# Two transformer-like layers on one core: layer 0's pairs of query tiles in another order on fixed PSUM banks, norms by a power, strips without fills, and the last pair's tail written out

## The chip, the cores and the metric

The kernel runs on one core of a Trainium2 chip, in fp32. The core has a matrix engine (TensorE, "PE"), a vector engine ("DVE"), an activation engine ("ACT"), a general engine ("POOL") and a queue engine ("SP") that issues most DMAs. Each engine works through its own instructions in order. Matmul results land in PSUM, which this kernel uses as eight banks of 128x512 floats. The metric is device time in microseconds (us); lower is better.

## The reference

The input x has shape (4, 2048, 256): four sequences of 2048 tokens. Two layers follow one another, each on a layer norm of its input and each added to that input.

```python
xn = _layernorm(x, axis=-1)
x = x + _L0_attn_ref(xn, ...) + _L0_ffn_ref(xn, ...)
xn = _layernorm(x, axis=-1)
x = x + _L1_attn_ref(xn, ...) + _L1_ffn_ref(xn, ...)
```

- The layer norm subtracts the mean and divides by sqrt(variance + 1e-5).
- Layer 0, first part: a gated linear recurrence along time, with a[t] and b[t] from two sigmoid gates of xn.
- Layer 0, second part: a router takes the mean over time of xn @ Wr + br, a softmax, and picks 4 of 16 heads (head size 64). For these four heads it computes full softmax attention over the 2048 keys (queries, keys and values scaled by the gate g), and multiplies by Wo.
- Layer 1, first part: causal attention with 16 heads of size 16 over 2048 tokens, then W_o.
- Layer 1, second part: a channel mix, sigmoid(xr @ W_r^T) * (relu(xk @ W_k^T)^2 @ W_v^T), where xr and xk mix a token with the one before.

## The kernel before

The four sequences (batches) are computed one after another. Every engine's program order is the order in which the Python code issues instructions; no planner moves them. The code interleaves work by generators: `steps(stream, n)` runs a stream n yields further. The streams are `recurring` (the recurrence, called `background` inside `attention0`), `projecting` (queries and keys of the next head), `rest_of_values` (values of layer 0), `norming` (the norm that layer 1 reads), `opening` (projections and strips of layer 1) and `leading` (row maxima of layer 1).

**Banks.** `own_bank` hands the eight banks out in turn. While `summing` is on, bank 7 is left out, because the weighing of layer 0 accumulates in it. A matmul that gets a bank must wait until the last reader of that bank is done.

**Layer 0's attention** (`attention0`) loops over 32 pairs of query tiles of 128 tokens (4 heads, 8 pairs each) plus two extra rounds that finish the last pairs. A pair has two tiles, a and c. For each tile:
- `scores` (L498): four matmuls (eight instructions in the trace, which shows two for each but a transpose) of 64 rows against 512 keys, two at a time on the two halves of the array, into four banks; DVE takes the maximum of each bank (L502) and joins them, negated, to `nm` (L506);
- `exponentials` (L512): ACT computes exp(score - max) of each bank into `p`, and sums rows on the way;
- `turn` (L520): PE transposes p, sixteen 128x128 blocks into four banks; `keep` (L526) copies each bank to `pT`, two on DVE and two on ACT;
- `weigh` (L545): for both tiles together, 64 instructions of pT with the values, in two halves (`weigh(0)`, `weigh(1)`) into bank 7; `weighed` (L552) copies the result on ACT;
- `project` (L558) multiplies by Wo, and `add` (L563) adds to x on DVE, divided by the row sum.

These steps are spread over rounds of the loop: in round n the code turns tile c of pair n-1 (`late`), projects pair n-2 (`older`), computes the scores of pair n, weighs pair n-1 and turns tile a of pair n. The order of a round is: late's turn, project, a's scores, c's first half of scores, weigh half, c's second half, weigh half, a's turn. The first round of a batch also computes values (L446) and the last steps of the recurrence: `added` (L330) on DVE, and transposes of y (L337) which are added to x.

**Norms** (`Norm`): `stats` (L257, L258 on DVE) per tile; `root` (L261) takes a square root on ACT; `inverse` (L265) a reciprocal on DVE; `rows` (L272) normalizes on DVE; `turn` (L278) transposes on PE and copies (L279). The norm of layer 1 runs inside `attention0` from the last head's pair 3 on, in blocks of four tiles (`all_blocks`), and ends in the two extra rounds and the eight rounds after them. The norm of the next batch runs inside layer 1 (`prepared`). [...]

**Layer 1** keeps q and k of four heads in a "strip": a tile with head h at partitions 32h to 32h+15. `open` (L711) fills a q strip with zeros and a k strip with ones on POOL; `copy` (L717) copies 16 rows per head by DMA. Row 16 of each head of the q strip later gets the negated row maximum by DMA, and meets a row of ones in k, so the matmul itself subtracts the maximum. `Maxima` (L772, L775, L778) compute row maxima of scores; `Weights` (L797 scores, L799 exp, L802 causal mask on POOL, L808 weighing, L814 copy, L815 sum on POOL) the attention, with a division of the result at L891 on POOL. `Leading.lead` issues one unit of four maxima.

## Time and profile before

| what | us |
|---|---|
| runs: median (lowest to highest of three) | 4234.19 (4233.68 to 4235.58) |
| profiled execution, own time | 4234.65 |
| its span in the trace | 4232.9 |
| first pair of layer 0 of each batch begins (L498) | 99.8, 1145.9, 2189.4, 3233.5 |
| PE busy | 4129.7 (98%) |
| DVE busy | 3107.5 (73%) |
| ACT busy | 2797.4 (66%) |
| POOL busy | 1044.9 (25%) |
| period of an ordinary pair of layer 0 | 11.82 |

Busy time is the sum of an engine's own instructions. A timeline row gives a start and a length in us, the engine, the line of the kernel, the operation with output <- inputs and the shape, and how many instructions the row stands for; in brackets comes the idle time before it and what ended it. Matmuls of different rows of the array overlap, so a row's length may be more than the distance to the next start. A row of waits gives the waiting instruction, what it waited for, the total in us, how often, and the longest. A row of windows gives for each engine the busy us and number of instructions, then the granted clock of PE as a share of full speed.

### The profile page before, as it was taken

To read this page: it belongs to the slowest core of one execution; us is meant where nothing else is said; L and a number is where in the kernel's file an instruction comes from. 1 tells how busy PE (TensorE), PEld (TensorE's weight loads), DVE (VectorE), ACT (ScalarE), POOL (GpSimd) and SP (SyncE) were. 2 spreads that over 40 slices of the span, in tenths; PEclk is the share of its full clock that TensorE was granted. 3 is DMA by queue.
4 is the path that set the end of the run, shared out by engine and by line. 5 is a ranking of instruction groups with operands and counts; after the bars stand their busy time and mean duration, and the time that the engine had idled before them with its cause. 6 is when DMAs were issued, how large, how long until landed. Compare 5 with 4: busy or idle time off the path is not lost.

```text
span 4232.9 us, 86387 instructions
## 1 busy us (share of the span) xinstructions
PE 4129.7 (98%) x32994; PEld 2283.5 (54%) x32994; DVE 3107.5 (73%) x7292; ACT 2797.4 (66%) x6388; POOL 1044.9 (25%) x1322
## 2 busy tenths in 40 slices
PE   6999999999999999999999999999999999999998
PEld 3777643334477764333457776433446777643334
DVE  5777778887577777888657776888856767688882
ACT  3666648886566665888656665688865666568874
POOL 0000015544100002654410000265440000036544
PEclk9999999999999999999999999999999999999999
DMA  3000010100100001110010000011000000001000
GB/s 87 1 11 1 6 18 17 19 25 17 27 1 11 1 6 19 17 37 6 19 25 1 11 1 9 16 17 37 7 19 23 1 11 1 16 11 17 16 7 24
DMA packets 70819, 65.80 MB, mean 16 GB/s; under 512 B 37234, under 2 KB 58628, under 8 KB 68868
## 3 DMA queue, kind: packets, MB, share of 16 engines
q1 hardware_dynamic: 66624, 57.19, 6.2%
q8 instruction: 260, 4.26, 0.4%
q10 hardware_dynamic: 3780, 3.07, 0.3%
q14 instruction: 155, 1.27, 0.1%
HBM read 16.70 MB, written 8.39 MB: 6 GB/s over the span
## 4 chain that ended last, share of the span: by engine, by line
PE 90%; DVE 5%; ACT 2%; issue 1%; POOL 1%; DMA 1%; ACTq 0%; SPq 0%; POOLq 0%; DVEq 0%
PE bank L797 15%; PE bank L772 13%; PE bank L808 12%; PE bank L520 11%; PE bank L498 10%; PE bank L545 10%; PE bank L993 4%; PE bank L703 3%; PE bank L294 3%; PE bank L558 2%; DVE mx L778 1%; PE bank L477 1%; PE bank L460 1%; PE bank L981 1%; DVE mx L502 1%; ACT p L512 1%
## 5 line engine op out<-in xcount | busy, mean ns | idle before, releaser
L799 ACT ACTIVATE p<-bank 128x512 f32<-128x512 f32 (+3 forms) x2560 | 1175.4, 540 | 281.1 <-PE bank L797 146.5
L772 PE MATMUL bank<-k,q 32*128 32x512 f32 (+3 forms) x5120 | 1139.1, 564 | 3.2 <-DVE mx L778 1.3
L778 DVE TENSOR_REDUCE mx<-bank 128x1 f32<-128x512 f32 x1536 | 952.9, 682 | 239.0 <-PE bank L772 238.6
L797 PE MATMUL bank<-q,k 32*128 32x512 f32 (+3 forms) x5120 | 1089.6, 555 | 0.0
L512 ACT ACTIVATE p<-bank,nm 128x512 f32<-128x512 f32 x1024 | 689.5, 685 | 568.6 <-DVE nm L506 568.5
L815 POOL TENSOR_TENSOR o<-o,w 128x512 f32<-128x512 f32 (+3 forms) x576 | 627.6, 1090 | 757.5 <-ACT w L814 752.0
L502 DVE TENSOR_REDUCE mx<-bank 128x1 f32<-128x512 f32 x1024 | 645.3, 681 | 94.8 <-PE bank L498 94.2
L797 PEld LDWEIGHTS bank<-q,k 32*128 32x128 f32 x5120 | 418.4, 184 | 533.7 <-ACT p L799 445.5
L808 PE MATMUL bank<-p,v 128*17 128x512 f32 (+3 forms) x5120 | 602.9, 534 | 16.6 <-POOL p L802 11.7
L526 DVE COPY pT<-bank 128x512 f32<-128x512 f32 x512 | 352.6, 691 | 293.2 <-PE bank L520 277.6
L545 PEld LDWEIGHTS bank<-pT,v 128*64 128x64 f32 x8192 | 441.9, 137 | 189.8 <-issue 189.3
L498 PE MATMUL bank<-k,q 64*128 64x512 f32 x2048 | 542.5, 611 | 0.8
L775 DVE CUSTOM_DVE_ANT_0 bank<-bank,cmask 128x512 f32<-128x512 f32 (+3 forms) x1024 | 473.3, 521 | 75.0 <-PE bank L772 56.4
L520 PE MATMUL bank<-ident,p 128*128 128x128 f32 x4096 | 492.3, 275 | 19.9 <-ACT p L512 19.7
L545 PE MATMUL bank<-pT,v 128*64 128x128 f32 x8192 | 503.7, 276 | 0.0
L772 PEld LDWEIGHTS bank<-k,q 32*128 32x128 f32 x5120 | 426.7, 183 | 136.7 <-DVE mx L778 34.5
L520 PEld LDWEIGHTS bank<-ident,p 128*128 128x128 f32 x4096 | 445.3, 141 | 73.8 <-ACT p L512 29.8
L711 POOL MEMSET q<- 128x2048 f32 x16 | 28.9, 1804 | 1659.5 <-PE bank L545 1659.5
L814 ACT COPY w<-bank 128x512 f32<-128x512 f32 (+3 forms) x576 | 305.1, 530 | 101.9 <-PE bank L808 68.4
L526 ACT COPY pT<-bank 128x512 f32<-128x512 f32 x512 | 293.4, 600 | 63.5 <-PE bank L520 61.5
L808 PEld LDWEIGHTS bank<-p,v 128*17 128x17 f32 x5120 | 89.7, 95 | 431.1 <-ACT p L799 235.8
L498 PEld LDWEIGHTS bank<-k,q 64*128 64x128 f32 x2048 | 210.5, 188 | 170.7 <-issue 84.9
(164 smaller groups left out, 3354.8 us busy)
## 6 DMA issues: line engine op xcount, KB each, us to landing
x<-in_L_attn_x_dram SPq DMA_DIRECT2D x20, 512.0 KB
q<-q SPq DMA_DIRECT2D x64, 128.0 KB
vals<-o SPq DMA_DIRECT2D x256, 32.0 KB
out_dram<-x SPq DMA_DIRECT2D x32, 256.0 KB
q<-qp SPq DMA_DIRECT2D x48, 128.0 KB
k<-kp SPq DMA_DIRECT2D x48, 128.0 KB
q<-nmT SPq DMA_DIRECT2D x256, 2.0 KB
q<-qp SPq DMA_DIRECT2D x64, 32.0 KB
```

Source lines behind the costliest of these rows:

```text
L498: PE.matmul(self.s[j][i], lhsT=self.qT[i][half_, self.t * P:(self.t + 1) * P], rhs=self.kT[half_, j * QB:(j + 1) * QB], start=True, stop=True)
L502: DVE.tensor_reduce(self.mx[:, n:n + 1], self.s[j][i], AX.X, ALU.max)
L512: ACT.activation(self.p[j][:, i, :], self.s[j][i], AF.Exp, bias=nm, accum_out=self.sums[:, n:n + 1])
L520: PE.transpose(self.tr[j][i][:, n * P:(n + 1) * P], self.p[j][:, i, n * P:(n + 1) * P], ident)
L526: copy(self.pT[:, n0:n0 + 4, :], self.tr[j][i].rearrange("p (n q) -> p n q", q=P))
L545: PE.matmul(acc[i * DH:(i + 1) * DH, 0:P], lhsT=self.v[h][:, N * j + n, self.k * DH:(self.k + 1) * DH], rhs=tile_.pT[:, 8 * h + N * j + n, ...
L772: PE.matmul(s[:, 0:n], lhsT=self.qT[strip(h), self.qs], rhs=self.kT[strip(h), self.ks], start=True, stop=True)
L778: DVE.tensor_reduce(self.mx[:, h, :], s[:, 0:n], AX.X, ALU.max)
L797: PE.matmul(s[:, c0:QB], lhsT=self.kT[strip(h), self.ks], rhs=self.qT[strip(h), self.q0 + c0:self.q0 + QB], start=True, stop=True)
L799: ACT.activation(p[:, h % 2, c0:QB], s[:, c0:QB], AF.Exp, scale=SC1)
L808: PE.matmul(acc[32 * h:32 * h + DH1 + 1, c0:QB], lhsT=self.v[h], rhs=self.p[h // 2][:, h % 2, c0:QB], start=True, stop=True)
L815: POOL.tensor_tensor(self.o[:, c0:QB], self.o[:, c0:QB], w[:, c0:QB], ALU.add)
```

## The change

The change has five parts.

1. *Norms by a power.* `root` and `inverse` become one step: DVE adds epsilon to the variance and POOL raises it to the power -0.5. The constant for epsilon goes; a constant of -0.5 comes. Over the whole program 39 of 58 table loads on ACT go.
2. *The router's mean.* The weight of 1/T becomes a tile of ones, and the factor 1/T moves into DVE's addition of the bias.
3. *Pairs in another order, on fixed banks.* `scores`, `turn`, `weigh` and `project` get their banks as arguments. Of late's four blocks of transposes, one comes first, and the other three between a's scores and c's scores. c's scores are no longer split, and the weighing is one run of 64 instructions into bank 0 after them. Late's four copies are all on ACT (before, two on DVE), which is 256 copies over the program. Streams that run inside a round are lent banks 6 and 4 at its start, and 4 and 7 at its end (1 and 3 in the first round). The first round runs no background step; values run two blocks and two blocks. The norm gets four steps per round; `all_blocks` has other yields.
4. *The last pair's tail.* The two extra rounds become straight code after the loop. In it, the maxima of layer 1 are issued as one unit, two units, and eight units in a loop, 11 in all before layer 1 begins (13 before), and the norm's steps stand among them.
5. *Strips without fills.* The maxima read 16 rows of a strip and the weights 17, instead of 32. POOL's fills go (32 of 1.8 us); the ones of the k strips come by DMA from the tile of ones, ahead of the copies (28 DMAs over the program).

```diff
@@ -112,10 +112,14 @@
-    turn, summing = [0], [False]
+    turn, summing, lent = [0], [False], []
...
+        if lent:
+            lent.append(lent.pop(0))
+            return banks[lent[-1]]
@@ -140,15 +144,15 @@
-    mean_w = const.tile([P, P], FP, tag="mean_w", name="mean_w")
-    POOL.memset(mean_w, 1.0 / T)
+    ones = const.tile([P, P], FP, tag="ones", name="ones")
+    POOL.memset(ones, 1.0)
...
-    eps_c = const.tile([P, 1], FP, tag="eps", name="eps_c")
-    POOL.memset(eps_c, EPS)
+    minus_half = const.tile([P, NT], FP, tag="minus_half", name="minus_half")
+    POOL.memset(minus_half, -0.5)
@@ -257,12 +261,10 @@
-        def root(self, t, n):
-            ACT.activation(self.rs[:, t:t + n], self.mv[:, t:t + n, 1:2].rearrange("p n o -> p (n o)"),
-                           AF.Sqrt, bias=eps_c)
...
-            DVE.reciprocal(self.rs[:, t:t + n], self.rs[:, t:t + n])
+            rs = self.rs[:, t:t + n]
+            DVE.tensor_scalar(rs, self.mv[:, t:t + n, 1:2].rearrange("p n o -> p (n o)"), EPS, None, ALU.add)
+            POOL.tensor_tensor(rs, rs, minus_half[:, 0:n], ALU.pow)
@@ -354,9 +356,9 @@
-            PE.matmul(ps[:, 0:NH], lhsT=mean_w, rhs=ws[:, c, :], start=(c == 0), stop=(c == 1))
+            PE.matmul(ps[:, 0:NH], lhsT=ones, rhs=ws[:, c, :], start=(c == 0), stop=(c == 1))
...
-        DVE.tensor_tensor(dist, ps[:, 0:NH], br_b, ALU.add)
+        DVE.scalar_tensor_tensor(dist, ps[:, 0:NH], 1.0 / T, br_b, ALU.mult, ALU.add)
@@ -491,8 +493,8 @@
-        def scores(self, j):
-            self.s[j] = [bank() for _ in range(2)]
+        def scores(self, j, to):
+            self.s[j] = to
@@ -501,29 +503,28 @@
-        def exponentials(self, js):
-            nm = sm.tile([P, 1], FP, tag="nm0", name=f"nm0_{self.name}")
-            DVE.tensor_reduce(nm, self.mx, AX.X, ALU.max, negate=True)
+        def maximum(self):
+            self.nm = sm.tile([P, 1], FP, tag="nm0", name=f"nm0_{self.name}")
+            DVE.tensor_reduce(self.nm, self.mx, AX.X, ALU.max, negate=True)
...
-            for j in js:
...
+        def exponentials(self, j, i):
+            if j not in self.p:
...
-                for i in range(2):
-                    n = 2 * j + i
-                    ACT.activation(self.p[j][:, i, :], self.s[j][i], AF.Exp, bias=nm,
-                                   accum_out=self.sums[:, n:n + 1])
...
-        def turn(self, j):
...
-            self.tr[j] = [bank() for _ in range(2)]
-            for i in range(2):
-                for n in range(4):
-                    PE.transpose(self.tr[j][i][:, n * P:(n + 1) * P], self.p[j][:, i, n * P:(n + 1) * P], ident)
+            n = 2 * j + i
+            ACT.activation(self.p[j][:, i, :], self.s[j][i], AF.Exp, bias=self.nm, accum_out=self.sums[:, n:n + 1])
...
+        def turn(self, j, i, to):
...
+            self.tr[j, i] = to
+            for n in range(4):
+                PE.transpose(to[:, n * P:(n + 1) * P], self.p[j][:, i, n * P:(n + 1) * P], ident)
...
-            copy(self.pT[:, n0:n0 + 4, :], self.tr[j][i].rearrange("p (n q) -> p n q", q=P))
+            copy(self.pT[:, n0:n0 + 4, :], self.tr[j, i].rearrange("p (n q) -> p n q", q=P))
@@ -537,22 +538,22 @@
-        def weigh(self, j):
-            acc, N = banks[7], NT // 4
-            for n in range(N):
+        def weigh(self, acc):
+            self.acc = acc
+            for n in range(NT // 2):
...
-                                  lhsT=self.v[h][:, N * j + n, self.k * DH:(self.k + 1) * DH],
-                                  rhs=tile_.pT[:, 8 * h + N * j + n, :], start=(j == n == h == 0),
-                                  stop=(j == h == 1 and n == N - 1))
+                                  lhsT=self.v[h][:, n, self.k * DH:(self.k + 1) * DH],
+                                  rhs=tile_.pT[:, 8 * h + n, :], start=(n == h == 0),
+                                  stop=(h == 1 and n == NT // 2 - 1))
...
-            ACT.copy(self.o, banks[7][:, 0:P])
...
-        def project(self):
-            self.ps = [bank() for _ in range(2)]
+            ACT.copy(self.o, self.acc[:, 0:P])
...
+        def project(self, to):
+            self.ps = to
@@ -562,6 +563,14 @@
+        def share(self):
+            for tile_ in self.tiles:
+                tile_.share()
...
+        def stats(self, norm):
+            for tile_ in self.tiles:
+                norm.stats(tile_.t)
@@ -569,33 +578,39 @@
         older, before = None, None
-        summing[0] = True
...
                 yield
-                norm.root(4 * q, 4)
-                yield
                 norm.inverse(4 * q, 4)
+                yield
                 norm.rows(q, 0, 2)
...
                     norm.turn(q, c, ACT.copy)
-                    yield
-                yield
-                yield
-        for n in range(NA * NP + 2):
+                    if q == NQ - 1:
+                        yield
+                yield
+                yield
+                yield
+                yield
+        def lend(*which):
+            lent[:] = which
+        def of(*which):
+            return [banks[i] for i in which]
+        for n in range(NA * NP):
             k, i = divmod(n, NP)
-            if i == 0 and 0 < k < NA:
+            if i == 0 and k:
                 steps(projecting, 100)
                 qk = following
-            new = Pair0(b, k, i, *qk, v, xt) if k < NA else None
-            a, c = new.tiles if new else (None, None)
+            new = Pair0(b, k, i, *qk, v, xt)
+            a, c = new.tiles
             if i == NP - 3 and k + 1 < NA:
@@ -606,82 +621,106 @@
-            steps(background, 1)
+            late = before.tiles[1] if before else None
+            lend(6, 4)
+            if n:
+                steps(background, 1)
             steps(projecting, 1)
...
-            if n in (NA * NP - 3, NA * NP - 1) or n >= NA * NP:
+            if n in (NA * NP - 3, NA * NP - 1):
                 steps(opening, 2)
-            if n >= NA * NP:
-                leading.lead()
+            lend()
             if before:
-                late = before.tiles[1]
-                late.turn(1)
-                late.turn(0)
-                late.keep(1, 0, DVE.tensor_copy)
-                late.keep(0, 0, DVE.tensor_copy)
-                late.keep(0, 1, ACT.copy)
+                late.turn(1, 1, *of(7))
                 late.keep(1, 1, ACT.copy)
-                for tile_ in before.tiles:
-                    tile_.share()
-            steps(background, 1)
+            if older:
+                older.project(of(3, 2))
+            if before:
+                before.share()
+            if older:
+                older.add()
+                if n - 2 >= (NA - 1) * NP:
+                    older.stats(norm)
+            steps(norming, 1)
+            a.scores(0, of(0, 5))
+            a.scores(1, of(4, 7))
+            a.maximum()
+            if before:
+                for j, i, to in ((0, 0, 1), (0, 1, 3), (1, 0, 6)):
+                    late.turn(j, i, *of(to))
+                    late.keep(j, i, ACT.copy)
+            else:
+                lend(1, 3)
+                steps(rest_of_values, 2)
+                lend()
+            for j, i in ((0, 0), (1, 1), (1, 0), (0, 1)):
+                a.exponentials(j, i)
+            steps(norming, 1)
+            c.scores(1, of(2, 1))
+            c.scores(0, of(3, 6))
+            c.maximum()
+            if before:
+                before.weigh(banks[0])
+            c.exponentials(0, 0)
+            c.exponentials(1, 1)
+            if before:
+                before.weighed()
+            c.exponentials(1, 0)
+            c.exponentials(0, 1)
+            lend(4, 7)
+            steps(rest_of_values, 2)
+            if n:
+                steps(background, 1)
             steps(projecting, 1)
             steps(norming, 1)
-            if older:
-                older.project()
-                older.add()
-                if n - 2 >= (NA - 1) * NP:
-                    for t in range(2):
-                        norm.stats(2 * (n - 2 - (NA - 1) * NP) + t)
-            if before and new is None:
-                leading.lead()
-            if new:
-                a.scores(0)
-                a.scores(1)
-                a.exponentials((0, 1))
-                steps(rest_of_values, 4)
-            steps(norming, 1)
-            if new:
-                c.scores(1)
-            if n >= NA * NP:
-                steps(opening, 1)
-            if before:
-                if new is None:
-                    leading.lead()
-                before.weigh(0)
-            if new:
-                c.scores(0)
-                c.exponentials((1, 0))
-            if before:
-                if new is None:
-                    leading.lead()
-                before.weigh(1)
-            if new:
-                a.turn(1)
-                a.turn(0)
-                a.keep(1, 0, DVE.tensor_copy)
-                a.keep(0, 0, DVE.tensor_copy)
-                a.keep(1, 1, ACT.copy)
-            if before:
-                before.weighed()
-            if new:
-                a.keep(0, 1, ACT.copy)
-            steps(norming, 1)
+            lend()
+            for j, i, to, copy in ((0, 0, 5, DVE.tensor_copy), (1, 0, 3, DVE.tensor_copy),
+                                   (1, 1, 0, ACT.copy), (0, 1, 1, ACT.copy)):
+                a.turn(j, i, *of(to))
+                a.keep(j, i, copy)
             older, before = before, new
...
+        summing[0] = True
+        steps(norming, 1)
+        steps(opening, 2)
+        leading.lead()
+        late = before.tiles[1]
+        for j, i in ((1, 1), (0, 0), (0, 1), (1, 0)):
+            late.turn(j, i, own_bank())
+            late.keep(j, i, ACT.copy)
+        older.project([own_bank() for _ in range(2)])
+        before.share()
+        older.add()
+        older.stats(norm)
+        steps(norming, 1)
+        for _ in range(2):
+            leading.lead()
+        steps(norming, 1)
+        before.weigh(banks[7])
+        before.weighed()
+        steps(norming, 1)
+        steps(opening, 1)
+        before.project([own_bank() for _ in range(2)])
+        before.add()
+        before.stats(norm)
+        steps(norming, 4)
+        steps(opening, 3)
         summing[0] = False
         for _ in range(8):
-            steps(opening, 1)
             leading.lead()
             steps(norming, 1)
+            steps(opening, 1)
         steps(norming, 100)
...
-    def strip(h):
-        return slice(32 * h, 32 * h + 32)
+    def strip(h, rows):
+        return slice(32 * h, 32 * h + rows)
@@ -706,11 +745,11 @@
-            t = half_tile(f"{'qk'[i]}1_{self.b}_{g}")
-            self.strips.setdefault(g, []).append(t)
-            POOL.memset(t, (0.0, 1.0)[i])
+            self.strips.setdefault(g, []).append(half_tile(f"{'qk'[i]}1_{self.b}_{g}"))
...
+            n = (blk.stop - blk.start) // P
+            SP.dma_start(self.strips[g][1][DH1:P:32, blk].rearrange("h (a r) -> h a r", r=P), ones[0:4 * n, :])
@@ -769,7 +808,7 @@
-            PE.matmul(s[:, 0:n], lhsT=self.qT[strip(h), self.qs], rhs=self.kT[strip(h), self.ks],
+            PE.matmul(s[:, 0:n], lhsT=self.qT[strip(h, DH1), self.qs], rhs=self.kT[strip(h, DH1), self.ks],
@@ -794,8 +833,8 @@
-            PE.matmul(s[:, c0:QB], lhsT=self.kT[strip(h), self.ks],
-                      rhs=self.qT[strip(h), self.q0 + c0:self.q0 + QB], start=True, stop=True)
+            PE.matmul(s[:, c0:QB], lhsT=self.kT[strip(h, DH1 + 1), self.ks],
+                      rhs=self.qT[strip(h, DH1 + 1), self.q0 + c0:self.q0 + QB], start=True, stop=True)
@@ -1024,9 +1063,8 @@
-            norm.root(0, NT)
+            norm.inverse(0, NT)
...
-            norm.inverse(0, NT)
```

## The prediction

> **What bounds the kernel now.** I read the page's busy times and its chain first, then TensorE's (PE's) waits, then timelines around the largest ones.
>
> ```profile
> PE 4129.7 (98%) x32994; PEld 2283.5 (54%) x32994; DVE 3107.5 (73%) x7292; ACT 2797.4 (66%) x6388; POOL 1044.9 (25%) x1322
> ...
> PE 90%; DVE 5%; ACT 2%; issue 1%; POOL 1%; DMA 1%; ACTq 0%; SPq 0%; POOLq 0%; DVEq 0%
> ```
>
> PE is busy for 98% and makes 90% of the chain. So an edit counts only where it removes PE time or PE waiting. The waits that belong to the changed code:
>
> ```profile
> PE bank L520 <- ACT p L512: 19.7, 16, 1.3
> PE bank L337 <- DVE y L330: 18.9, 4, 4.7
> PE bank L808 <- POOL p L802: 11.7, 20, 1.3
> ```
>
> (us in total, times, longest.) The first two are 38.6 us. The 4.7 us wait comes once per batch, in the first pair:
>
> ```profile
> 1144.92 1.09 PE L337 MATMUL bank<-ident,y 128*128 128x128 f32 x4 [4.73 <-DVE y L330]
> 1145.93 3.78 PE L498 MATMUL bank<-k,q 64*128 64x512 f32 x8
> 1149.64 7.17 PE L446 MATMUL bank<-wv,xT 128*128 128x256 f32 x32
> 1156.75 1.99 PE L498 MATMUL bank<-k,q 64*128 64x512 f32 x8
> ...
> 1161.45 0.66 PE L520 MATMUL bank<-ident,p 128*128 128x128 f32 x4 [1.25 <-ACT p L512]
> ```
>
> Eight L498 matmuls take 3.78 us here and 1.99 us ten us later. The windows (the last columns are granted clock, DMA share, GB/s) say why: the clock falls to about half after the wait.
>
> ```profile
> 1140.00:1145.00 5.00, 0.27 (x2) 0.12 (x2) 4.96 (x5) 0.38 (x1) 0.00 (x0) 0.78 0.00 0
> 1145.00:1150.00 5.00, 5.00 (x14) 2.12 (x15) 3.20 (x5) 0.00 (x0) 0.00 (x0) 0.54 0.01 3
> 1278.30:1302.00 23.70, 23.70 (x236) 17.59 (x236) 18.38 (x41) 15.62 (x43) 0.00 (x0) 1.00 0.00 1
> ```
>
> The last row is two ordinary pairs: PE never idles, full clock, 11.82 us a pair. The late pairs have stalls from the norm's square root, which stands between two tiles' exponentials:
>
> ```profile
> 1502.49 1.28 ACT L261 ACT_TABLE_LOAD   x1
> 1503.79 0.30 ACT L261 ACTIVATE rs<-mv,eps_c 128x4 f32<-128x4 f32 x1
> 1504.10 1.28 ACT L512 ACT_TABLE_LOAD   x1
> ```
>
> **Start of a batch (pair 0): 6.5 us gained, four times.** The late steps of recurrence (the L330 adds and the first L337 block) leave pair 0. Before, PE was done with earlier values at 1140.2 and reached pair 1's scores at 1165.35: 25.2 us. After, the same stretch by the rows: a's scores 1140.2–1142; then two blocks of values on banks 1 and 3, held until DVE's copy of the previous block has emptied one: that copy starts at 1142.91 (the scan on DVE is ahead of it) and takes 0.67, so a new wait of 1.6; values to 1147.1 (half of 7.17); c's scores to 1149; a wait of 0.4 for bank 4, which a's third exponential reads; values to 1153; a's turn to 1154.9. That is 14.7, 10.5 less, but work is only put off: 12 late transposes (1.3) and three L337 blocks that pair 0 held (1.5 with their switches). 7.7 remain, of which 4.7 is the wait and 1.9 the half clock (3.78 less 1.99, if a 1.6 us wait doesn't lower it) and the rest the 1.25. As the put-off L337 blocks cost something in later pairs, I take 6.5: 26 in all. Bounds per batch: 3 (half clock kept and one more us waited) and 8.
>
> **Pairs 26 to 31 and the tail: 9 us gained, four times.** A pair with norm steps but no root lasts 0.94 longer than its work; a pair with a root 2.1 longer than that (1.23 wait plus the second group of c's scores, which took 2.29 instead of 1.24). Six pairs with statistics 1.05 each and three with roots 2.1 each: 12.5 us. After, ACT has no root: DVE adds epsilon, POOL takes the power and both are a step ahead of the rows (L272). The pair has a new price: two tiles' statistics (0.42+0.18+0.39+0.18, slots 1.08) stand on DVE ahead of a's maxima; L506 ends 1.08 later, so does the first exponential, which must empty bank 0 before the weighing may start. With 0.6 of slack (below) this is 0.45 a pair, 2.7. Gain 9.8. In the tail the changed order puts the last statistics and turns between maxima, but five units of maxima run with little between: DVE takes 4x0.617=2.47 for each, PE 1.14 a unit; against this the two extra rounds' waits (4.9 before) go. I book a loss of 1: 9 remain, 36 in all (bounds 16 and 46).
>
> What does the power cost? No row has it. Nearest is a POOL TENSOR_TENSOR: 1.09 us mean at 128x512, 0.45 at 128x128; here it is 128x4 (128x16 in the next batch's norm). Bounds: 0.1, a tiny memset on POOL, and 1.1, as if size were nothing. I take 0.4. In the pairs about 3 us lie between it and the rows, so even 1.1 is hidden; in the tail 1.5. If POOL were behind other work by more, DVE's rows and the maxima behind them would wait; POOL does nothing in those pairs.
>
> [...] The build has 39 loads fewer. [...]
>
> **Ordinary pairs: 0.05 us gained, 100 times.** The same 32 transposes, 32+32 weighing, 16 scores, 4 projections are in another order. Rows of one old pair (the projections' 0.54 follow):
>
> ```profile
> 1290.15 2.74 PE L498 MATMUL bank<-k,q 64*128 64x512 f32 x12
> 1292.83 1.97 PE L545 MATMUL bank<-pT,v 128*64 128x128 f32 x32
> 1294.72 1.24 PE L498 MATMUL bank<-k,q 64*128 64x512 f32 x4
> 1295.89 1.97 PE L545 MATMUL bank<-pT,v 128*64 128x128 f32 x32
> 1297.79 3.71 PE L520 MATMUL bank<-ident,p 128*128 128x128 f32 x32
> ```
>
> The new groups by the same spacings: late transpose group, project and a's scores 2.35; twelve late transposes 1.46 and switches; c's scores 1.9; one weighing of 64 in a row 3.65; a's sixteen 1.9. The sum is 11.71 to 11.83, by how one books the switches. [...] Scores, weighing and transposes have three shapes, and transposes now stand between scores. [...]
>
> Fixed banks mean waits. I walked each bank with durations from the timeline (copy 0.60 on ACT, 0.69 on DVE, exponential slot 0.66, max slot 0.617, 0.17 from PE to a reader). With 0 at the pair's start: bank 1 is free 4.1, wanted by c's scores 4.3; bank 6, 5.05 against 5.3; bank 0, 5.6 against 6.25; bank 0 again (weighed) 10.4 against 10.8; bank 7, 1.4 against 1.9. So nothing stalls, but margins are 0.25 to 0.6. The copies moved to ACT (256, 2 a pair at 0.48) lie under PE: ACT is then busy 8.3 of 11.7, DVE 7.7. If the cover is gone, late's third copy delays c's second scores. I take 0.05 x 100 = 5, bounds +11 and -30.
>
> **The rest: nothing.** Strips with 16 and 17 rows instead of 32: the stationary load and the stream go by columns, and a 512-column score takes 0.59 from 32 rows (L772) and 0.61 from 64 (L498), so rows hardly count. The 32 memsets:
>
> ```profile
> 723.11 1.81 POOL L711 MEMSET k<- 128x2048 f32 x1
> 726.64 1.26 POOL L815 TENSOR_TENSOR o<-o,w 128x512 f32<-128x512 f32 x1 [1.71 <-ACT w L814]
> ```
>
> After one, POOL idles 1.71: 58 us leave an engine that waits. The L808 wait (11.7) follows a multiplication (L891), which stays. [...] Mean as a factor in DVE's add: the same instruction count.
>
> **Sum.** 26 + 36 + 5 = 67. The profiled execution took 4234.65, its span 4232.9, and the median of the runs is 4234.19: no correction. 4234 - 67 = 4167; I say 4166.
>
> **Rivals.** (a) *Half of the gain is lost in ordinary pairs*: a bank margin of 0.25 fails by about 0.3: 100 x 0.3 = 30, so about 4200. For it: I allowed 0.17 for a hand-over, and DVE's copies in the late pairs show one of 0.35. Against it: the copy that frees the bank is one instruction with steady duration.
> (b) *Slower*: a loop closes through ACT. Late's copies, all four on ACT, stand ahead of a's exponentials; if a late one is held until c's last exponential of the pair before is through, a's exponentials, the weighing and c's exponentials slip, and the next pair begins with the slip. It decides from 67/128 = 0.52 us a pair; one exponential and its read (0.66) is enough for 128 x 0.66 = 84 less 67: 4251. For it: ACT's order is strict and c's last exponential ends 0.3 before the pair does. Against it: ACT has 3.4 us of idle time per pair to catch up.
> (c) *No change*: the waits move but remain. Pair 0 waits for DVE's scan in another place (6.5 becomes 1), and the weighing waits for statistics as long as for roots. About 4230. Against it: the scan is followed by a copy that needs no more than 0.67.
>
> **Chances and range.** Forecast (gain 40 to 110) 0.70; (a), with gains of 10 to 40, 0.12; (b) 0.14; (c) 0.04. Range: below, all upper bounds together (6 + 10 + 6 = 22) give 4144, and 0.1 less per changed mode switch 10 more: 4135. Above, (a) reaches 4194 to 4224; cut at 4215 it leaves out (b), (c) and a sixth of (a), 0.2 in all. The forecast's own range is 4135 to 4194. 0.2% (8.5 us) is about what a measurement can tell from no change: faster 0.82, same 0.04, slower 0.14.
>
> **What would show it.** Right: no L337 row with over 2 us before it in a batch's first pair; no table load in pairs 26–31; PE without idle time in ordinary pairs at 11.7–11.85; the weighing (its new line) waiting about 0.5 for an exponential in pairs 26–31. Wrong: PE rows of transposes, c's scores or weighing with a wait for an ACT copy or exponential in every pair, which is (a) up to 0.5 and (b) above; the granted clock at half in new places; maxima waiting for rows behind the power.

## The result: 26% slower, at half the clock through layer 1

The changed kernel takes 5328.57 us (5324.99 to 5328.83, four runs) against 4234.77 us beside it: a ratio of 1.258, 95% interval 1.256 to 1.260. The forecast was 4166. The page of its profile, its span first (PEclk is the granted clock in 40 slices, tenths of full speed):

```profile
span 5323.3 us, 86113 instructions
...
PE 5248.2 (99%) x32994; PEld 2554.4 (48%) x32994; DVE 2970.6 (56%) x7036; ACT 2947.0 (55%) x6585; POOL 1018.4 (19%) x1310
...
PEclk9999655557999955555899995555589999555558
...
L811 PE MATMUL bank<-k,q 16*128 16x512 f32 (+3 forms) x5120 | 1921.5, 929 | 4.1 <-DVE mx L814 3.6
L836 PE MATMUL bank<-q,k 17*128 17x512 f32 (+3 forms) x5120 | 1909.3, 922 | 0.0
...
L847 PE MATMUL bank<-p,v 128*17 128x512 f32 (+3 forms) x5120 | 1007.8, 871 | 12.1 <-POOL p L841 5.9
```

The same rows of the kernel before:

```profile
PEclk9999999999999999999999999999999999999999
...
L772 PE MATMUL bank<-k,q 32*128 32x512 f32 (+3 forms) x5120 | 1139.1, 564 | 3.2 <-DVE mx L778 1.3
L797 PE MATMUL bank<-q,k 32*128 32x512 f32 (+3 forms) x5120 | 1089.6, 555 | 0.0
...
L808 PE MATMUL bank<-p,v 128*17 128x512 f32 (+3 forms) x5120 | 602.9, 534 | 16.6 <-POOL p L802 11.7
```

PE issues as many instructions as before (32994) and is busier than before (99%), but those of layer 1's attention are longer: the maxima (before L772, now L811) take 929 ns instead of 564, the weights' scores (L797, now L836) 922 instead of 555, the weighing (L808, now L847) 871 instead of 534. The last of these was not edited at all. The row of the clock shows what went with it: four stretches at half speed, one per batch. Their ends are in the trace's clock record (570.0 and 1262.9 us for the first); a window laid on the first shows PE busy for all of it but 1.4 us:

```profile
570.00:1262.90 692.90, 691.46 (x3392) 226.29 (x3390) 354.11 (x865) 340.71 (x704) 198.19 (x265) 0.50 0.05 10
```

So the time went into layer 1, and not into waits. Layer 0, which most of the edit and of the forecast was about, became shorter. The first pair of the second batch, then two ordinary pairs:

```profile
1410.43 1.99 PE L500 MATMUL bank<-k,q 64*128 64x512 f32 x8
1413.94 3.72 PE L448 MATMUL bank<-wv,xT 128*128 128x256 f32 x16 [1.52 <-DVE v L450]
1417.59 2.04 PE L500 MATMUL bank<-k,q 64*128 64x512 f32 x8
1420.09 3.72 PE L448 MATMUL bank<-wv,xT 128*128 128x256 f32 x16 [0.45 <-ACT p L515]
1423.64 2.35 PE L521 MATMUL bank<-ident,p 128*128 128x128 f32 x20
1425.92 1.99 PE L500 MATMUL bank<-k,q 64*128 64x512 f32 x8
```

```profile
201.00:224.40 23.40, 23.40 (x235) 17.60 (x233) 15.73 (x37) 17.51 (x46) 0.00 (x0) 1.00 0.01 2
```

No row before the first pair waits for DVE's y, the eight scores take 1.99 us (full clock), and two ordinary pairs are 23.40 us without idle time at full clock: 11.70 each. PE's waits in the late pairs (first row: total us, times, longest) and in the first pairs of the batches are small and regular:

```profile
PE bank L546 <- ACT p L515: 9.0, 24, 0.4
PE bank L448 <- DVE v L450: 6.1, 4, 1.5
```

From the first to the last score of layer 0 a batch now takes 404.3 us instead of 420.2.

### The profile page after: what moved, and what is told of

It reads as the page before. It is cut to its first block, busy times and chain, and to the rows that moved or that the text cites. A ratio compares the mean times of both kernels' runs of the same rounds, so it can differ in the third digit from the quotient of the medians.

```text
span 5323.3 us, 86113 instructions
## 1 busy us (share of the span) xinstructions
PE 5248.2 (99%) x32994; PEld 2554.4 (48%) x32994; DVE 2970.6 (56%) x7036; ACT 2947.0 (55%) x6585; POOL 1018.4 (19%) x1310
## 4 chain that ended last, share of the span: by engine, by line
PE 94%; DVE 3%; ACT 1%; POOL 0%; DMA 0%; issue 0%; ACTq 0%; SPq 0%; POOLq 0%; DVEq 0%
PE bank L836 20%; PE bank L847 18%; PE bank L811 17%; PE bank L546 9%; PE bank L521 8%; PE bank L500 7%; PE bank L1032 3%; PE bank L742 2%; PE bank L296 2%; PE bank L559 1%; PE bank L1020 1%; PE bank L771 1%; PE bank L462 1%; DVE mx L504 1%; PE bank L479 1%; PE bank L280 1%
## 5 line engine op out<-in xcount | busy, mean ns | idle before, releaser
L811 PE MATMUL bank<-k,q 16*128 16x512 f32 (+3 forms) x5120 | 1921.5, 929 | 4.1 <-DVE mx L814 3.6
L836 PE MATMUL bank<-q,k 17*128 17x512 f32 (+3 forms) x5120 | 1909.3, 922 | 0.0
L838 ACT ACTIVATE p<-bank 128x512 f32<-128x512 f32 (+3 forms) x2560 | 1215.4, 535 | 1062.8 <-PE bank L836 576.0
L836 PEld LDWEIGHTS bank<-q,k 17*128 17x128 f32 x5120 | 704.8, 302 | 859.8 <-ACT p L838 744.9
L847 PE MATMUL bank<-p,v 128*17 128x512 f32 (+3 forms) x5120 | 1007.8, 871 | 12.1 <-POOL p L841 5.9
L811 PEld LDWEIGHTS bank<-k,q 16*128 16x128 f32 x5120 | 733.7, 302 | 402.1 <-issue 344.5
L504 DVE TENSOR_REDUCE mx<-bank 128x1 f32<-128x512 f32 x1024 | 634.5, 682 | 69.6 <-PE bank L500 69.6
L527 ACT COPY pT<-bank 128x512 f32<-128x512 f32 x768 | 405.3, 598 | 301.9 <-PE bank L521 301.9
L500 PE MATMUL bank<-k,q 64*128 64x512 f32 x2048 | 496.4, 603 | 0.0
L847 PEld LDWEIGHTS bank<-p,v 128*17 128x17 f32 x5120 | 99.5, 109 | 735.7 <-ACT p L838 472.8
L527 DVE COPY pT<-bank 128x512 f32<-128x512 f32 x256 | 164.8, 685 | 293.6 <-PE bank L521 287.9
L841 POOL TENSOR_SCALAR_AFFINE_SELECT p<-p 128x256 f32<-128x256 f32 x512 | 208.6, 413 | 542.5 <-ACT p L838 540.9
```

Source lines behind the costliest of these rows:

```text
L500: PE.matmul(self.s[j][i], lhsT=self.qT[i][half_, self.t * P:(self.t + 1) * P], rhs=self.kT[half_, j * QB:(j + 1) * QB], start=True, stop=True)
L504: DVE.tensor_reduce(self.mx[:, n:n + 1], self.s[j][i], AX.X, ALU.max)
L527: copy(self.pT[:, n0:n0 + 4, :], self.tr[j, i].rearrange("p (n q) -> p n q", q=P))
L811: PE.matmul(s[:, 0:n], lhsT=self.qT[strip(h, DH1), self.qs], rhs=self.kT[strip(h, DH1), self.ks], start=True, stop=True)
L836: PE.matmul(s[:, c0:QB], lhsT=self.kT[strip(h, DH1 + 1), self.ks], rhs=self.qT[strip(h, DH1 + 1), self.q0 + c0:self.q0 + QB], start=True, ...
L838: ACT.activation(p[:, h % 2, c0:QB], s[:, c0:QB], AF.Exp, scale=SC1)
```

## The experiments

A run with one number was timed once; where a range stands, four or five times. Two theories stood at the start. R: the clock follows how many rows of the array work, so part 5 (strips of 16 and 17 rows) halves it. O: the order, the power or the tail of layer 0 brings PE into a low clock that it then keeps.

**Part 5 undone, and part 5 alone.** The first kernel is the changed one with strips of 32 rows, filled on POOL; the second is the kernel before with shorter slices and nothing else.

```diff
-            self.strips.setdefault(g, []).append(half_tile(f"{'qk'[i]}1_{self.b}_{g}"))
+            t = half_tile(f"{'qk'[i]}1_{self.b}_{g}")
+            self.strips.setdefault(g, []).append(t)
+            POOL.memset(t, (0.0, 1.0)[i])
...
-            SP.dma_start(self.strips[g][1][DH1:P:32, blk].rearrange("h (a r) -> h a r", r=P), ones[0:4 * n, :])
...
-            PE.matmul(s[:, 0:n], lhsT=self.qT[strip(h, DH1), self.qs], rhs=self.kT[strip(h, DH1), self.ks],
+            PE.matmul(s[:, 0:n], lhsT=self.qT[strip(h, 32), self.qs], rhs=self.kT[strip(h, 32), self.ks],
...
```

> The changed kernel with part 5 alone undone: strips of 32 rows again, fills on POOL, no DMAs of ones. Theory R: the clock of the matrix engine is granted by how many of its rows work, not by how long it is busy, so the 16- and 17-row matmuls of layer 1 halve it. Then this run has a granted clock of 0.99 and takes 4160 us (4145 to 4185): 4234 less the 15.9 us per batch that the stretch from the first to the last score of layer 0 became shorter (420.2 to 404.3) and some 10 more. Rival O: the new order, the power or the new tail of layer 0 put the engine into a low clock that it does not leave. Then the time stays near 5320 and the clock near 0.74.

> The kernel before with only the rows that the matmuls of layer 1 read cut from 32 to 16 (maxima) and 17 (weights); fills, order, norms as before. Theory R: half clock through layer 1's attention; it becomes about 290 us longer per batch (770.7 against 480.8 from its first to its last weights score), 1160 in all: 5390 us (5300 to 5450), clock 0.74. Rival O: 4234 us and clock 0.99.

Measured: 4169.26 us (4168.31 to 4170.64; ratio to before 0.985, interval 0.983 to 0.986), granted clock 0.994; and 5395.51 us, granted clock 0.743. Part 5 alone makes the kernel before slower by 1162 us; without it the change is a gain of 64.6 us. O is out. In the first run the clock is full through layer 1's attention:

```profile
585.00:1055.00 470.00, 466.40 (x3814) 194.12 (x3812) 378.54 (x920) 365.18 (x796) 244.00 (x305) 1.00 0.08 19
```

**One of the two matmuls short.** As the first kernel, with `strip(h, 16)` in the maxima alone, or `strip(h, 17)` in the weights' scores alone.

> As the first run, but the maxima read 16 rows; the weights 32. If the clock follows the mean of working rows over a window, the mean lies between the two (maxima and weights take about the same time, and the weighing has full rows), and the run shows on which side of the limit it falls: either half clock in all of the attention (over 5000 us) or in the short stretch of maxima alone before the weights (10 us per batch, half clock, about 4190 us). If any short-row matmul holds the clock down: over 5000 us. Rival O: no difference from the first run.

> As the first run, but the weights' scores read 17 rows; the maxima 32. By the mean of rows the same as the run with maxima of 16 rows, but the stretch of maxima alone keeps its full rows, so the half clock begins later if at all: 4165 us or over 5000. Rival O: no difference from the first run.

Measured: 4215.38 us, clock 0.979; 4166.17 us, clock 0.993. So in these two runs a short row count in one of the matmuls did not hold the clock down through layer 1. With short maxima the record shows half clock for 17 to 31 us from the stretch of maxima alone on, then full clock, and in three batches 10 to 14 us of half clock again at a block on the diagonal; with short weights 10 us. And at full clock the shorter shape did not make the instruction longer: 622 ns against 621. Of L836 with 512 elements, by shape, first with 32 rows, then with 17 rows at full clock, then with 17 rows in the changed kernel, where most of them ran at half:

```profile
L836 PE MATMUL bank<-q,k 32*128 32x512 f32 x3584 | 863.6, 621 | 0.0
```

```profile
L836 PE MATMUL bank<-q,k 17*128 17x512 f32 x3584 | 866.6, 622 | 0.0
```

```profile
L836 PE MATMUL bank<-q,k 17*128 17x512 f32 x3584 | 1528.3, 1044 | 0.0
```

**Theory C.** C is an estimate of mine, worked out from the clock records and the matmul records of these runs. In the traces of the two kernels the boundaries between full and half clock are whole multiples of 3.41 us apart (the 692.9 us above are 203 of them). For each such window I added up, over the matmul records that start in it, rows x columns x streamed elements, divided by 128 x 128. The changed kernel's windows at half clock after which it stayed at half have a median of 968 and at most 1144, and the eight after which it rose have 1792 to 2048; the first rise, at 1262.87 us, follows the window in which the channel mix begins (L1020 at 1260.47, all rows and columns). In the kernel before, five windows at half clock that stayed have 1024 to 1536, and the six that rose 1536 to 2048. In all runs so far but the one with short maxima, windows after which the clock rose had 1430 or more; in that run some counted 930, and I can't tell missing records from a softer limit. Rows x elements without the columns (divided by 128) do not sort the windows: some of the changed kernel with up to 4696 of those (the weighing has 128 rows but 17 columns) did not lift the clock, and some of the kernel before with 1536 did. So C supposes that a window at half clock needs some 1200 to 1500 of this sum before the clock rises. If so, there is a consequence: at half clock the same work per window is half as much. Work of 970 at half clock would be 1940 at full, over the estimate. It would keep a full clock, but could not get one back.

> As the run with 32 rows, but both matmuls of layer 1's scores read 24 rows (fills on POOL cover them). Theory C, in place of the plain count of rows: a window of 3.41 us of the trace's clock record is judged by rows x columns x streamed elements; in the runs so far no window at half clock went to full below about 1430 to 1540 of the unit 128x128 cells x elements, and the changed kernel's windows at half clock have a median of 968. With 24 rows this median is 968 x (0.75+0.75+0.53)/(0.5+0.53+0.53) = 1260, the same as with maxima of 16 rows and weights of 32. So the clock should behave as there: half after the stretch of maxima alone and then back in some tens of us: 4190 to 4400 us. A theory by which any short row count halves the clock: over 5000 us. One by which 24 rows are enough: 4166 us.

Measured: 4204.55 us, clock 0.982; half clock after the stretch of maxima for 17 to 31 us, and in three batches for 13.7 us at the first weak block on the diagonal. The time is in C's range, and neither of the others fits. But some windows of this run after which the clock rose count only 1040 to 1272, so the estimate above does not hold as it stands.

**Zeros in the rows.** The 32-row kernel with `POOL.memset(t, 0.0)` for both strips and the one row of ones by DMA, as part 5 does it.

> As the run with 32 rows, but the k strips are filled with zeros (the row of ones comes by DMA as in the changed kernel), so rows 17 to 31 multiply zero by zero. Theory C: rows count whatever they hold: 4168 us (4155 to 4185), clock 0.99. Rival D, the clock follows the data that toggles in the array: as the changed kernel, over 5000 us, clock near 0.74.

Measured: 4164.43 us, clock 0.996. With zeros times zeros in 15 of the 32 rows the time and the clock are those of the 32-row kernel (4169.26 us, 0.994) and not those of the changed one (5328.57 us, 0.738); D is out, and so are the DMAs of the ones, which this run has too.

**A burst in the changed kernel.** If C is right, the changed kernel needs only to be lifted once.

```diff
         while leading.count < 4 * NQ + 4:
             leading.lead()
             steps(opening, 1)
+        for _ in range(6):
+            PE.matmul(own_bank(), lhsT=ident, rhs=xT[0][:, 0:QB], start=True, stop=True)
```

> The changed kernel (16 and 17 rows) with six additional matmuls of 128 rows, 128 columns and 512 elements, whose result nothing reads, per batch just before layer 1's loop (about 12 us at half clock). Theory C with a latch: at full clock the same work is twice as much per window, about 1940, over the limit, so after the burst the clock is full and stays so until a weak window (blocks on the diagonal, a wait of PE of a us), and then is half until the next dense stretch: tens of us of full clock per batch, 5200 to 5320 us. Theory L (the level alone, no latch): half again one or two windows after the burst: 5330 to 5350 us.

Measured: 5041.43 us, clock 0.796: 287 us less than the changed kernel, for more work. Windows of its first batch (the clock is the third column from the end):

```profile
576.00:579.40 3.40, 3.40 (x5) 1.51 (x5) 2.10 (x4) 0.00 (x0) 0.00 (x0) 0.50 0.00 0
579.40:582.80 3.40, 3.40 (x9) 1.33 (x7) 0.00 (x0) 0.00 (x0) 0.00 (x0) 0.99 0.00 0
582.80:650.00 67.20, 67.08 (x586) 26.87 (x585) 55.58 (x144) 53.39 (x121) 30.42 (x44) 1.00 0.08 14
650.00:722.80 72.80, 72.33 (x636) 28.54 (x632) 61.35 (x154) 60.95 (x133) 38.69 (x52) 1.00 0.08 15
722.80:726.20 3.40, 2.37 (x32) 1.25 (x28) 1.98 (x12) 1.29 (x5) 3.40 (x6) 1.00 0.02 5
726.20:729.60 3.40, 3.40 (x18) 1.21 (x16) 1.28 (x2) 1.46 (x3) 3.10 (x6) 0.51 0.00 0
...
733.00:1160.00 427.00, 426.17 (x2088) 132.73 (x2080) 217.89 (x526) 212.21 (x435) 117.92 (x154) 0.50 0.05 12
```

After the burst the clock is full for 147 us with nothing but 16- and 17-row scores and weighing (about 1730 by C's count in the window of 716.1 to 719.5 us), and it falls after the window of 722.9 to 726.3 us, of 911: a diagonal block in which PE also waits for POOL's mask:

```profile
725.27 0.97 PE L847 MATMUL bank<-p,v 128*17 128x256 f32 x8 [1.03 <-POOL p L841]
```

Then the same work stays at half for 437 us. The same kind of work ran at both clocks in one batch, full after the burst and half after the fall, which is what C with a latch expects. The size was missed: I expected full clock for tens of us; it held 147 in three batches, and two windows in the fourth.

**The maxima earlier.** By C a smaller loss in the 32-row kernel would have the same cause: five units of maxima in a row before layer 1, where DVE sets the pace (2.48 us a unit, for which PE needs 1.14 at full clock). Four of them are moved among the projections.

```diff
-        for _ in range(8):
+        for r in range(8):
             leading.lead()
             steps(norming, 1)
             steps(opening, 1)
+            if r in (3, 5, 7):
+                leading.lead()
...
-        steps(opening, 2)
+        steps(opening, 1)
+        leading.lead()
+        steps(opening, 1)
```

> The run with 32 rows, and four of the five units of maxima that stood one after another before layer 1's loop are issued earlier, one after every second step of the projections. Theory C: the stretch in which PE works less than half the time (each unit 1.1 us of PE beside 2.48 of DVE) is gone, and with it the 6.8 us of half clock per batch: 3.4 for the clock and about 1.4 a unit for the waiting, 9 per batch, 36 in all, if the projections' PE time covers DVE: 4133 us (4125 to 4155). Rival: the earlier maxima only put DVE's work in front of other maxima, and the time does not change: 4165 to 4172.

> The changed kernel (16 and 17 rows) with the same earlier maxima. Theory C with a latch: the weak stretch that lets the clock fall at 570 us is gone, so the clock stays full until the next weak window, a diagonal block about 155 us later (it fell there at 726 in the run with the burst), and then is half until a dense stretch: as the run with the burst less its cost, 5025 us (4950 to 5080). A theory by which rows alone set the clock: 5300 us.

Measured on 32 rows: 4152.33 us (4150.59 to 4156.39; ratio 0.981, interval 0.980 to 0.982), clock 0.997: faster than both kernels of this study. The window of 573.3 to 576.7 us, in the 32-row kernel and then in this one:

```profile
573.30:576.70 3.40, 3.40 (x12) 2.97 (x13) 3.40 (x11) 0.00 (x0) 0.00 (x0) 0.50 0.00 0
```

```profile
573.30:576.70 3.40, 3.40 (x21) 1.42 (x20) 2.05 (x6) 1.76 (x4) 0.00 (x0) 1.00 0.00 0
```

The half clock is gone there, but the gain is 17 us and not 36. The forecast had two parts. Half clock between the last scores of layer 0 and the first weights' scores went from 29 us in the program to 7; I estimate its worth at half of those 22 us. The other part, 1.4 us of waiting for each of 16 units, mostly did not come; why is open. On 16 and 17 rows: 5314.99 us, a miss for my number; it is near the 5300 of the rival by which rows alone set the clock, and it is the run with the burst that speaks against that one. The clock fell at 580.9 instead of 570: the window of 577.5 to 580.9 us, in the first blocks of layer 1 before any weighing, has 1180 by C's count. So the earlier maxima put the fall off by 11 us and did not prevent it.

**Fewer maxima ahead.** On 32 rows, `while leading.count < 4 * NQ + 2`.

> As the run with 32 rows, but the maxima run 18 units ahead of the weights instead of 20, so two units fewer are issued one after another with nothing between them just before layer 1's loop, where DVE takes 2.48 us a unit and the clock record shows 6.8 us of half clock per batch. Per batch: two units of 2.48 become 1.1 each beside weights (2.7), and half the slow stretch goes (3.4): 6 x 4 = 24 us: 4145 us (4135 to 4160). Rival: the weights of a block now wait for the maxima's row, which comes by DMA: 4170 us or more.

Measured: 4193.29 us (4190.35 to 4194.9), 24 us slower than with 20: my forecast had the sign wrong. What it was about came true: over the four batches the stretch before the weights became 23 us shorter. But the attention behind it became 45 us longer, which the forecast left out (in the first batch weights begin at 572.7 instead of 576.8 and take 492 us instead of 479). The weighing now waits for ACT, first the row with 18 units ahead, then with 20:

```profile
PE bank L847 <- ACT p L838: 18.0, 52, 0.5
PE bank L847 <- ACT p L838: 3.7, 12, 0.3
```

Each unit of maxima stands beside another unit of weights, so small maxima meet other weights; that this makes the waits is not shown. They are 14 us of the 45, and the rest I did not trace. It is not the clock: half clock is 51.4 us of the program in both (granted clock 0.994 in both).

**The power undone.** On 32 rows, with a square root on ACT and a reciprocal on DVE at the place where the new order has the power.

```diff
-            DVE.tensor_scalar(rs, self.mv[:, t:t + n, 1:2].rearrange(...), EPS, None, ALU.add)
-            POOL.tensor_tensor(rs, rs, minus_half[:, 0:n], ALU.pow)
+            ACT.activation(rs, self.mv[:, t:t + n, 1:2].rearrange(...), AF.Sqrt, bias=eps_c)
+            DVE.reciprocal(rs, rs)
```

> The run with 32 rows with part 1 undone at the place where the new order has it: a square root on ACT and a reciprocal on DVE in place of DVE's addition and POOL's power. If the table loads (2.91 us between exponentials) are what the power removes, c's exponentials in three pairs and the tail of each batch come 2.9 later, of which PE feels 1.2 to 2.4: 16 x 1.8 = 29 us more: 4198 us (4185 to 4220). If the order alone already hides them: 4169 us; less, down to 4160, if the power on POOL costs the tail more than the loads do.

Measured: 4240.05 us, 71 us more. Without the power the new order is no faster than the kernel before. The wait, then ACT and PE in one such pair:

```profile
PE bank L521 <- ACT p L515: 50.9, 12, 4.2
```

```profile
479.64 1.28 ACT L266 ACT_TABLE_LOAD   x1
480.94 0.30 ACT L266 ACTIVATE rs<-mv,eps_c 128x4 f32<-128x4 f32 x1
484.09 1.28 ACT L515 ACT_TABLE_LOAD   x1 [2.85 <-DVE nm L508]
485.38 0.69 ACT L515 ACTIVATE p<-bank,nm 128x512 f32<-128x512 f32 x1
```

```profile
486.21 2.82 PE L521 MATMUL bank<-ident,p 128*128 128x128 f32 x12 [4.24 <-ACT p L515]
488.83 1.31 PE L280 MATMUL bank<-ident,xn 128*128 128x128 f32 x8
```

The second load does not use the 2.85 us in which ACT is idle: it starts only when c's maximum is there. The transposes (12 in 2.82 us) then also pay for a low clock: the record has half clock from 485.96 us on, for 3.4 us. The same twelve take 1.53 at full clock.

**What C's sum sorts.** In the traces of the two kernels, the rises: of 827 windows at half clock, the 813 that stayed have at most 1536 and the 14 that rose at least 1536. Not in all runs: in those with 24 rows, with the burst and with the maxima earlier, windows of 1040 to 1300 lifted the clock, and in those with short maxima or 24 rows some of over 1500 did not. The fall is sorted less well: the 14 windows of the two kernels after which the clock fell have at most 1216, but twelve below that kept it, five of 868 to 1158 in the kernel before and seven of 510 to 1071 in the changed one; PE also waits 1.1 us for POOL in one of these, at 1344.8 us of the changed kernel with 714. So C stays an estimate from these runs, and none of them shows what sets the granted clock.

## Why the prediction was wrong

**The step that failed** is "The rest: nothing", in its first sentence: "Strips with 16 and 17 rows instead of 32: the stationary load and the stream go by columns ... so rows hardly count." As a statement on durations at full clock it holds (621 and 622 ns for L836 with 32 and 17 rows; in the kernel before, stationary loads of 128 columns took 183 ns from 32 rows, L772, and 188 from 64, L498, and one of 17 columns from 128 rows 95, L808). But I costed part 5 only by an instruction's duration, and never asked what it does to the granted clock, though I had the clock in the windows. I had read its fall at 1140 as the price of an idle PE. In layer 1 of the changed kernel it was at half with PE busy for 691.46 of 692.90 us, so idle time alone does not account for it; little work in a window, as C has it, is my estimate. The runs put part 5 at 5328.6 - 4169.3 = 1159 us. By the record, 4 x 692.9 = 2772 us ran at half clock; the same work at full takes 2772 - 1159 = 1613, so it became longer by 1.72 and not by 2; I take the rest to be time that other engines set, which no run measured.

None of the rivals had this: (a) to (c) all looked for waits in layer 0. The forecast's list of what would prove it wrong had "the granted clock at half in new places"; that is where it showed.

**What held**, by the 32-row kernel, in which all other parts stand:
- The sum: 67 us forecast, 64.6 measured. That it is so near is in part luck, as two misses cancel. Up to the last scores of layer 0 the gain was 77 us where I had 70, and the tail lost 15 where I had 4 (both with 8 us put back, for weighing that now stands behind those scores).
- Start of a batch: the stretch from PE's last value to the next pair's scores was worked out at 14.7 us, and is 15.5 (1410.4 to 1425.9); the new waits at 1.6 and 0.4, and are 1.52 and 0.45; the half clock there is gone.
- Ordinary pairs: I took 11.77; they are 11.70, at the end of the range of 11.71 to 11.83 that assigns least to switches. The bound of 30 us on the loss there, and the 0.1 us a mode switch at the lower end of the range, are shown by no run: with five shape changes a pair in both orders, two pairs took 23.40 us with PE busy for 23.40. No bank waits, though one margin of my walk was 0.2 (bank 1: free at 4.1, wanted at 4.3) and not 0.25.
- Late pairs: the weighing waits 0.38 in 24 pairs, forecast 0.45. The five periods from pair 26 on were 77.1 us before and are 69.6.

**What was off in size.** The tail: I booked a loss of 1 per batch. From the last score of layer 0 to the first weights' score it was 74.7 us and is 78.3 to 81.6, so 4 to 7. About 2 of that is weighing that only moved (128 of its instructions stand there now, 94 before). The rest goes with the clock: the stretch has 3.7 to 9.3 us of half clock and had none before, 12 of the program's 29 us at the five units of maxima, which I had named. The power: I took 0.4, with 1.1 as the bound as if size were nothing. In the changed kernel, by shape:

```profile
L267 POOL TENSOR_TENSOR rs<-rs,minus_half 128x4 f32<-128x4 f32 x16 | 16.1, 1009 | 1847.2 <-DVE rs L266 1847.2
L267 POOL TENSOR_TENSOR rs<-rs,minus_half 128x16 f32<-128x16 f32 x4 | 11.7, 2928 | 24.3 <-DVE half_b L197 24.2
```

With 4 columns it is just inside, with 16 far outside: an addition's row was no bound for a power. I had also misread that row: 1.09 is the mean of the addition over four sizes, and at 128x512 it takes 1.27. In the pairs it is hidden all the same; in the tail DVE waits 1.12 for it. And what the power is worth was undersized: I priced its absence by the old order's waits (1.23), but in the new order the loads would cost 4.2 a pair.

Two smaller figures were off without consequence. ACT is busy 8.76 us of an ordinary pair's 11.70 (17.51 in two), not 8.3: 7.81 before and two copies of 0.48 more is 8.77 already. And 0.59 for a 32-row score is the length of single rows; the mean of that shape is 626 ns, and 611 with 64 rows.

## What to carry to other kernels

The granted clock is part of an instruction's price: the 17-row score of 512 elements took 622 ns on average in one run and 1044 in another. After making matmuls smaller, read the granted clock of the stretch and not only busy time. Here strips of 16 and 17 rows went with a clock of 0.738 and strips of 32 rows with 0.994, and with 0.996 where 15 of the rows held only zeros. Look as well at a run of work that another engine paces, such as the units of maxima alone (half clock from 573.3 to 576.7 us in the 32-row kernel). When an instruction's duration is taken from a row, ask at which clock that row ran and whether the edit leaves it there.

## What was not expected of the hardware

- PE shown as busy for 691.46 of 692.90 us in the changed kernel, and granted 0.50 of the clock all the same.
- The same kind of work at two clocks: 147 us at full and 437 us at half in one batch of the run with the burst.
- Rows of zeros went with the full clock: 32 rows, 15 of them zero times zero, 4164.43 us against 5328.57 with 16 and 17.
- POOL's power: 1.01 us for 4 columns and 2.93 us for 16, by estimate from the two 0.16 us a column, against 1.27 us for an addition of 512 columns.
- In the run with the square root, a table load in front of an activation that waits began only after the wait (484.09 us, 2.85 us unused).

Left open: what sets the granted clock, why some windows of little work did not lower it, and what columns have to do with it, since no run changed them.
